# A long convolution and Haar mixing kernel: a place within the tick for each engine's part of a stage, and 14 instead of 12 products on ScalarE in the first mixing

## The chip, the cores and the metric

One core of a Trainium2 chip. The metric is the device time of the one launch in microseconds (us), the median of several runs. One execution is also recorded by the hardware profiler; all views below come from that execution.

## The reference, cut to what matters

The input is `x[4, 64, 256, 256]` in f32: 4 batches, 64 channels, images of 256 x 256. Four layers follow each other.

```
for layer in (0, 1):                       # a long convolution, each channel by itself
    k = outer(hx, hy)                      # 256 x 256 filter, from two small sine networks
    x = causal_conv2d(x, k) + x * bias     # (done by FFT in the reference)

f1  = haar2d(x)                            # layer 2: Haar transform of rows and columns
for i in (0, 1):                           # soft threshold of mixed coefficients
    f4  = conv_w[i] @ (f1 * v[i])          # mixes the 64 channels, at every position
    acc += sign(f4) * relu(abs(f4) - tau[i])
x   = haar2d_inverse(acc) + x

k   = outer(hx3, hy3)                      # layer 3: a long convolution again
out = causal_conv2d(x, k) + x * bias
```

The filter is an outer product, so a 2-D convolution is one product with a triangular Toeplitz matrix along each axis.

## The kernel before, in words

All work is cut into small stages. One **unit** of a convolution is one channel of one batch, a tile of 128 partitions x 2 x 256. Its stages are:

- `load`: the image and the first Toeplitz tile are fetched (issued on the queue of SyncE, SP).
- `a0`: `contract` multiplies with the Toeplitz matrix along one axis on TensorE into an accumulator `pa` (lines L190 and L191), and ScalarE copies the accumulator to `a` (L199).
- `y0`: the same along the other axis into `py`, and VectorE adds the input times the bias, the **residual sum** (L212).
- `a1`, `y1`: layer 1 in the same way. `a1` reads what the sum of `y0` wrote.
- `pairs`: the first Haar step on VectorE (L257, L258), into one of eight slots of `sd`; `store` sends that slot to DRAM (`keep`).
- `levels`: three events for every four channels, the remaining Haar levels along the row, in place in `sd` (VectorE, L269 and L270). The first of them overwrites what `store` reads.
- `split` and `down`: ScalarE and VectorE split the slot into two reduced-precision parts (L280, L281), TensorE applies the column transform (`pz`, L288), ScalarE copies the result (L296), and a DMA writes it to `coef`.

**Mixing** goes over 64 **groups** of 4 rows of coefficients for each batch. `mix` multiplies a group with the channel weights on TensorE (`px`, L340) into one of two accumulators and scales it by `v`. A group has 16 lines of 64 values; VectorE does the first `16 - n_act` of them in one instruction (L357), ScalarE the other `n_act`, one instruction each (L359). Then come `shrink` (ScalarE: Abs L365, Sign L366; VectorE: the subtraction of tau, L367), `signed` (VectorE: maximum with 0, times the sign, L372) and `add` (VectorE: the two products are added into `z`, L376). L367 and L372 are the **threshold steps**. `n_act` is 12 in the first three batches and 6 in the last.

**Inverse** goes over 64 channels: `fetch` (ScalarE gathers a channel of `z`, L396), `rows` (`pw` on TensorE, L403 and L404; ScalarE and VectorE split it, L406 and L407), `cols` (`pu`, L416; VectorE joins it with the kept image to `t` and `u`, L420 to L424), then layer 3 as `a3`, `y3` and the output DMA. A third of the channels of the first three batches is put off: `u` goes to DRAM (`late`), and its layer 3 is done during the last mixing (`convolution`).

The forward stages of the next batch are spread over the mixing of the present one, so a mixing stage holds both kinds of work. TensorE's work in such a tick is the product `px` and up to four contractions and one `pz`.

The order is set by a list of events: every stage of every unit has a tick, and within the tick a place.

```
    def at(tick, place, run, unit):
        events.append((tick, place, len(events), run, unit))
...
            for s, (place, stage) in enumerate([(-2.5, mix), (-3.5, shrink), (-4.1, signed), (-4.2, add)]):
                at(start + g + s, place, stage, g)
...
    for _, _, _, stage, unit in sorted(events, key=lambda e: e[:3]):
        stage(unit)
```

The sorted list is the order in which the instructions are handed to the framework. The framework keeps that as a priority; its planner may let an instruction that it takes to be ready go ahead of one that it takes to be waiting. The order on each engine is thus settled in the built program, and the engine then runs it strictly in that order, waiting where an operand is not there. Buffers are few: two accumulators for `px`, four for everything else on TensorE, two tiles each for the products `f4` and for `mag`, one for the split parts.

Of the kernel before, what the change touches and what calls it, by code (L numbers as in the profile page):

```python
# [9 lines left out]
F32 = mybir.dt.float32  # L10
# [7 lines left out]
P = 128  # L18
ROW = S + P

GT = 4
BUFS = {"res": 1, "y": 3, "co": 2}

INV_2PI = float(np.float32(1.0 / (2.0 * math.pi)))
MAGIC = float(1.5 * 2.0**23)
# [12 lines left out]
def conv_seq_kernel(ctx, tc, x, fz, fw, bias, decay, haar, haar_row, factors, vt, taut, wmix, out):  # L38
# [152 lines left out]
            nc.tensor.matmul(ps[:, m, P:], src[:, 1, m * P : (m + 1) * P], t[:, : P - 1 : -1], start=False, stop=True)  # L191

    def first(b, st, key, layer, new):
        def run(c):
            s = st[c]
            ps = bank(f"p{new}_{b}_{c}")
            contract(ps, s[key], s[layer][:, 0, :])
            a = io.tile([P, 2, S], F32, name=f"{new}_{b}_{c}", tag="mid")
            nc.scalar.copy(a, ps)  # L199
            s[new] = a  # L200

        return run

    def second(b, st, key, layer, res, new, tag, ahead=None):
        def run(c):
            s = st[c]
            if ahead is not None:
                s[ahead] = toeplitz(ahead, c, f"t{ahead}_{b}_{c}")
            ps = bank(f"p{new}_{b}_{c}")
            contract(ps, s[key], s[layer][:, 1, :])  # L210
            y = io.tile([P, 2, S], F32, name=f"{new}_{b}_{c}", tag=tag, bufs=BUFS[tag])
            nc.vector.scalar_tensor_tensor(y, s[res], bsb[:, layer, c : c + 1], ps, ALU.mult, ALU.add)  # L212
            s[new] = y

        return run

    def butterfly(b):

# [4 lines left out]

    events = []

    def at(tick, place, run, unit):
        events.append((tick, place, len(events), run, unit))

    def stream(stages, ticks):

        for unit, tick in enumerate(ticks):
            for s, stage in enumerate(stages):
                if stage is not None:
                    at(tick + s, -s, stage, unit)

    def convolutions(b, ticks, in_parts=(), border=None):

# [8 lines left out]
            nc.sync.dma_start(xt, x[b, c].rearrange("(k p) w -> p k w", p=P))  # L248
            st[c] = {"x": xt, 0: toeplitz(0, c, f"t0_{b}_{c}")}

        last_second = second(b, st, "a1", 1, "y0", "y1", "res")

        def pairs(c):
            last_second(c)
            v = st.pop(c)["y1"].rearrange("p k (w e) -> p k w e", e=2)
            t = sd[:, c % 8]
            nc.vector.tensor_add(t[:, :, 0, :], v[:, :, :, 0], v[:, :, :, 1])  # L257
            nc.vector.tensor_sub(t[:, :, 1, :], v[:, :, :, 0], v[:, :, :, 1])  # L258
# [17 lines left out]
        def split(c):  # L276

            w = parts[c] = mx.tile([P, 2, 2, S], F32R, name=f"sp_{b}_{c}", tag="sp", bufs=1)
            t = sd[:, c % 8].rearrange("p k e w -> p k (e w)")
            nc.scalar.copy(w[:, 0], t)  # L280
            nc.vector.tensor_tensor(w[:, 1], t, w[:, 0].bitcast(F32), ALU.subtract)  # L281

        def down(c):
            ps = bank(f"pz_{b}_{c}")
            flat = "p k w -> p (k w)"
            if c in in_parts:
                for i in range(2):
                    nc.tensor.matmul(  # L288
                        ps.rearrange(flat), hbr, parts[c][:, i].rearrange(flat), start=(i == 0), stop=(i == 1)
                    )  # L290
            else:
                nc.tensor.matmul(
                    ps.rearrange(flat), hbt, sd[:, c % 8].rearrange("p k e w -> p (k e w)"), start=True, stop=True
                )
            t = io.tile([P, 2, S], F32, name=f"co_{b}_{c}", tag="co", bufs=BUFS["co"])
            nc.scalar.copy(t, ps)  # L296
            nc.sync.dma_start(coef[b][:, c].rearrange("k p w -> p k w"), t)

        stream(
            [load, first(b, st, "x", 0, "a0"), second(b, st, "a0", 0, "x", "y0", "y", ahead=1), first(b, st, "y0", 1, "a1"), pairs],  # L300
            ticks,
        )
        for c, tick in enumerate(ticks):

            at(tick + 4, 3, store, c)
        for n in range(C // 4):
            end = ticks[4 * n + 3] + 4
            for s, steps in enumerate([(1,), (2, 4), (8, 16, 32, 64)]):
                at(after(end + 1 + s, n), 1, levels(steps), n)
            for j in range(4):  # L310
                if 4 * n + j in in_parts:
                    at(after(end + 3 + j, n), 2, split, 4 * n + j)
                at(after(end + 4 + j, n), 2, down, 4 * n + j)
        return after(ticks[-1] + 11, C // 4 - 1)

    def mixing(b, start, n_act):
# [18 lines left out]
        def mix(g):  # L335
            f = st[g]["f"]
            ps = psx.tile([P, 2, 2, S], F32, name=f"px_{b}_{g}", tag="mix")
            for q in range(2):
                for h in range(2):
                    nc.tensor.matmul(  # L340
                        ps[:, h, q, :],
                        f[:, q, h * P : (h + 1) * P],
                        wb.rearrange("p r n -> p (r n)"),
                        start=True,
                        stop=True,
                    )
            if g == 0:

                one, two = ps[:, :, 0, :P], ps[:, :, 0, P:]
                d = mx.tile([P, 2, P], F32, name=f"d_{b}", tag="mag")  # L350
                nc.vector.tensor_copy(d, two)
                nc.vector.tensor_sub(two, one, d)
                nc.vector.tensor_add(one, one, d)
            f4 = mx.tile([P, 16, C], F32, name=f"f4_{b}_{g}", tag="f4")
            px = ps.rearrange("p h q (r i o) -> p (h q r i) o", r=2, i=2)
            n = 16 - n_act
            nc.vector.tensor_tensor(f4[:, :n], px[:, :n], over(g, 0, n), ALU.mult)  # L357
            for j in range(n, 16):
                nc.scalar.mul(f4[:, j], px[:, j], scale(g, 0)[:, j : j + 1])  # L359
            st[g]["f4"] = f4  # L360

        def shrink(g):
            f4 = st[g]["f4"]
            mag = mx.tile([P, 16, C], F32, name=f"mag_{b}_{g}", tag="mag")
            nc.scalar.activation(mag, f4, AF.Abs)  # L365
            nc.scalar.activation(f4, f4, AF.Sign)  # L366
            nc.vector.tensor_sub(mag, mag, over(g, 1, 16))  # L367
            st[g]["mag"] = mag

        def signed(g):  # L370
            mag = st[g]["mag"]
# [4 lines left out]
            nc.vector.tensor_add(z[:, :, 4 * g : 4 * g + 4, :], parts[:, :, :, 0, :], parts[:, :, :, 1, :])  # L376

        for g in range(S // 4):
            at(start + g - 2, 0, load, g)

            for s, (place, stage) in enumerate([(-2.5, mix), (-3.5, shrink), (-4.1, signed), (-4.2, add)]):
                at(start + g + s, place, stage, g)

    def inverse(b, start, put_off):

# [11 lines left out]
        def rows(c):  # L399
            a = st[c]["z"]  # L400
            ps = psm.tile([P, 2, 2, P], F32, name=f"pw_{b}_{c}", tag="mm")
            for m in range(2):
                nc.tensor.matmul(ps[:, m, 0, :], a[:, 0, m, :], hsinv, start=True, stop=True)  # L403
                nc.tensor.transpose(ps[:, m, 1, :], a[:, 1, m, :], ident)  # L404
            w = mx.tile([P, 2, 2, 2, P], F32R, name=f"w_{b}_{c}", tag="f4")
            nc.scalar.copy(w[:, 0], ps)  # L406
            nc.vector.tensor_tensor(w[:, 1], ps, w[:, 0].bitcast(F32), ALU.subtract)  # L407
            st[c]["w"] = w
            if c not in put_off:
                st[c][2] = toeplitz(2, c, f"t2_{b}_{c}")  # L410

        def cols(c):
            ps = psm.tile([P, 2, 2, P], F32, name=f"pu_{b}_{c}", tag="mm")
            flat = "p m e w -> p (m e w)"
            for i in range(2):
                nc.tensor.matmul(  # L416
                    ps.rearrange(flat), hb, st[c]["w"][:, i].rearrange(flat), start=(i == 0), stop=(i == 1)
                )
            t = io.tile([P, 2, 2, P], F32, name=f"t_{b}_{c}", tag="res", bufs=BUFS["res"])
            nc.vector.scalar_tensor_tensor(t, st[c]["r"], 0.5, ps, ALU.mult, ALU.add)  # L420
            u = io.tile([P, 2, S], F32, name=f"u_{b}_{c}", tag="y", bufs=BUFS["y"])
# [2 lines left out]
            nc.vector.tensor_sub(v[:, :, :, 1], t[:, :, 0, :], t[:, :, 1, :])  # L424
            st[c]["u"] = u

        ends = last(b, st)
        for c in range(C):

            at(start + c, -1, fetch, c)  # L430
            at(start + c + 1, -9, rows, c)
            at(start + c + 2, -8, cols, c)
            if c in put_off:
                at(start + c + 3, -5, lambda c: nc.scalar.dma_start(late[b, c], st.pop(c)["u"]), c)
            else:
                for s, stage in enumerate(ends):
                    at(start + c + 3 + s, s - 7, stage, c)

    def last(b, st):
        return [  # L440
            first(b, st, "u", 2, "a3"),
            second(b, st, "a3", 2, "u", "y3", "co"),
            lambda c: nc.scalar.dma_start(out[b, c].rearrange("(k p) w -> p k w", p=P), st.pop(c)["y3"]),
        ]

    def convolution(which, ticks):

        for (b, c), tick in zip(which, ticks):
# [4 lines left out]
                nc.sync.dma_start(u, late[b, c])  # L453
                st[c] = {"u": u, 2: toeplitz(2, c, f"t2_{b}_{c}")}

            for s, stage in enumerate([load, *last(b, st)]):
                at(tick + s, -s, stage, c)


    def spread(begin, end, n=C):  # L460
# [17 lines left out]
    two[8](9)  # L478
    for tick, do in enumerate([constants, None, None, *three[:-1], *tables()], 4):
        if do is not None:  # L480
            at(tick, 3, lambda unit, do=do: do(), 0)

    groups = S // 4
    ready = convolutions(0, range(C), in_parts=range(C))
    ahead = C
    start = ready + 3
    for b in range(B):
        mixing(b, start, 12 if b + 1 < B else 6)
        end = start + groups + 3
        if b + 1 < B:  # L490
            ready = convolutions(b + 1, spread(ahead, end + 2), in_parts=range(C), border=end)
# [5 lines left out]

        start = max(end + C, ready + 3)
        ahead = start - 3
    for _, _, _, stage, unit in sorted(events, key=lambda e: e[:3]):  # L500
        stage(unit)


# [107 lines left out]
```

## Time and profile before

| | us |
|---|---|
| median of 3 runs | 2977.2 (2973.15 to 2978.07) |
| the profiled execution | 2975.2 |
| its span | 2973.4 |
| px of the first mixing begins | 453.5 |
| px of the last mixing ends | about 2708 |
| 453 to 883, first mixing and its border: PE, DVE, ACT busy | 418.93, 405.97, 390.40 of 430 |
| 1092 to 1558, second mixing | 460.27, 430.00, 404.26 of 466 |
| 1558 to 1766, second inverse | 207.03, 176.16, 137.86 of 208 |
| 2436 to 2725, last mixing | 280.28, 279.36, 245.02 of 289 |

PE is TensorE's matmuls, PEld its weight loads, DVE VectorE, ACT ScalarE, SP the queue of SyncE. "Busy" is the time in which at least one instruction of the engine runs; instructions that follow at once overlap at their ends, so a mean duration is longer than the step from one to the next. The granted TensorE clock is 1.00 throughout. In the waits, `A <- B: t, n, m` says that A's engine was idle for t us in n stretches, the longest m, until B released it.

### The profile page before, as it was taken

The page shows a single profiled execution, that of the slowest core. Times are in us where ns is not written, and L with a number is a line of the kernel's source. Part 1 is how long each engine was busy: PE and PEld are TensorE (multiplying, and loading weights), DVE is VectorE, ACT ScalarE, POOL GpSimd, SP SyncE. Part 2 cuts the span into 40 slices and gives each one's busy share as a digit, 9 for nine tenths or more (in the row PEclk, how much of TensorE's full clock was granted, in tenths as well). Part 3 has the DMA queues.
Part 4 walks back from the last instruction along what each step waited for, and adds up shares of the span by engine and source line. Part 5 has one row for each costly group of instructions (what it writes and reads, how often), then busy time and mean ns, then how long its engine had stood idle before and what let it go on. Part 6 is the DMA issues. An engine that isn't in the chain of part 4 may idle for free. (4 is left out here: it accounts for less than half of the span.)

```text
span 2973.4 us, 52066 instructions
## 1 busy us (share of the span) xinstructions
PE 2913.8 (98%) x16950; PEld 2615.1 (88%) x16950; DVE 2545.5 (86%) x4571; ACT 2156.9 (73%) x5014; POOL 0.2 (0%) x4
## 2 busy tenths in 40 slices
PE   8999999999999999999999999999999999999999
PEld 6898988888888898888888988888888988888998
DVE  5766768999998879999989879999998889998776
ACT  2333338999986758889986668989986768887554
POOL 0000000000000000000000000000000000000000
PEclk9999999999999999999999999999999999999999
DMA  5877777666667876776777876777777878777676
GB/s 159 247 237 226 229 228 212 203 202 207 207 196 244 250 217 200 208 216 204 208 219 244 250 225 197 209 210 211 207 216 237 256 236 235 233 230 217 212 212 186
DMA packets 562497, 649.73 MB, mean 219 GB/s; under 512 B 44369, under 2 KB 447412, under 8 KB 562100
## 3 DMA queue, kind: packets, MB, share of 16 engines
q1 hardware_dynamic: 482996, 562.07, 64.8%
q10 hardware_dynamic: 79232, 84.34, 8.0%
q8 instruction: 137, 2.24, 0.3%
q14 instruction: 132, 1.08, 0.1%
HBM read 426.77 MB, written 219.48 MB: 217 GB/s over the span
## 5 line engine op out<-in xcount | busy, mean ns | idle before, releaser
L190 PE MATMUL py<-t,a 128*128 128x256 f32 x3072 | 919.0, 381 | 8.9 <-ACT a L199 5.5
L199 ACT COPY a<-pa 128x512 f32<-128x512 f32 x768 | 477.2, 621 | 387.9 <-PE pa L191 357.2
L359 ACT ACTIVATE f<-px,vt 128x64 f32<-128x64 f32 x2688 | 582.3, 358 | 143.5 <-DVE f L357 143.4
L191 PEld LDWEIGHTS py<-t,a 128*128 128x128 f32 x3072 | 583.4, 190 | 79.3
L191 PE MATMUL py<-t,a 128*128 128x128 f32 x3072 | 590.0, 274 | 0.0
L190 PEld LDWEIGHTS py<-t,a 128*128 128x128 f32 x3072 | 500.4, 191 | 50.9 <-ACT a L199 12.4
L340 PE MATMUL px<-wb,f 128*128 128x256 f32 x2048 | 488.2, 380 | 4.9 <-ACT f L359 4.9
L340 PEld LDWEIGHTS px<-wb,f 128*128 128x128 f32 x2048 | 369.5, 190 | 47.0 <-ACT f L359 6.7
L367 DVE TENSOR_TENSOR mag<-mag,vt 128x1024 f32<-128x1024 f32 x256 | 312.4, 1220 | 28.3 <-ACT mag L365 26.9
L190 PE MATMUL pa<-t,y 128*128 128x256 f32 x1024 | 311.6, 386 | 22.4 <-DVE y L212 20.3
L406 ACT CAST w<-pw 128x512 fp32r<-128x512 f32 x256 | 150.2, 587 | 227.0 <-PE pw L404 218.9
L372 DVE SCALAR_TENSOR_TENSOR mag<-mag,f 128x1024 f32<-128x1024 f32 x256 | 311.7, 1218 | 1.9
L190 PE MATMUL pa<-t,x 128*128 128x256 f32 x1024 | 305.9, 380 | 0.4 <-issue 0.4
L365 ACT ACTIVATE mag<-f 128x1024 f32<-128x1024 f32 x256 | 293.7, 1147 | 11.0 <-DVE z L376 8.8
L366 ACT ACTIVATE f<-f 128x1024 f32<-128x1024 f32 x256 | 285.2, 1114 | 3.0
L396 ACT COPY zc<-z 128x512 f32<-128x512 f32 x256 | 282.0, 1103 | 0.7 <-ACT w L406 0.4
L281 DVE TENSOR_TENSOR sp<-sd,sp 128x512 fp32r<-128x512 f32 x256 | 176.1, 688 | 91.4 <-ACT sp L280 90.2
L190 PE MATMUL pa<-t,u 128*128 128x256 f32 x772 | 232.8, 383 | 2.9 <-PE pu L416 1.6
L420 DVE SCALAR_TENSOR_TENSOR t<-r,pu 128x512 f32<-128x512 f32 x256 | 174.9, 683 | 60.4 <-PE pu L416 57.0
L212 DVE SCALAR_TENSOR_TENSOR y<-x,bsb,py 128x512 f32<-128x512 f32 x256 | 190.1, 742 | 37.9 <-PE py L191 36.1
L212 DVE SCALAR_TENSOR_TENSOR y<-y,bsb,py 128x512 f32<-128x512 f32 x256 | 190.0, 742 | 34.2 <-PE py L191 33.1
L191 PEld LDWEIGHTS pa<-t,x 128*128 128x128 f32 x1024 | 194.6, 190 | 26.3
(67 smaller groups left out, 4458.9 us busy)
## 6 DMA issues: line engine op xcount, KB each, us to landing
t<-pad SPq DMA_DIRECT2D x768, 256.0 KB, 3.9
x<-in_x SPq DMA_DIRECT2D x256, 256.0 KB, 3.6
keep<-sd SPq DMA_DIRECT2D x256, 256.0 KB, 2.9
coef<-co SPq DMA_DIRECT2D x256, 256.0 KB, 3.3
f<-coef SPq DMA_DIRECT2D x256, 256.0 KB, 3.2
r<-keep SPq DMA_DIRECT2D x256, 256.0 KB, 3.3
out_y<-y ACTq DMA_DIRECT2D x256, 256.0 KB, 3.6
late<-u ACTq DMA_DIRECT2D x63, 256.0 KB, 2.9
```

The lines of the kernel that those rows point to most:

```text
L190: nc.tensor.matmul(ps[:, m, :], src[:, 0, m * P : (m + 1) * P], t[:, ::-1], start=True, stop=False)
L191: nc.tensor.matmul(ps[:, m, P:], src[:, 1, m * P : (m + 1) * P], t[:, : P - 1 : -1], start=False, stop=True)
L199: nc.scalar.copy(a, ps)
L212: nc.vector.scalar_tensor_tensor(y, s[res], bsb[:, layer, c : c + 1], ps, ALU.mult, ALU.add)
L281: nc.vector.tensor_tensor(w[:, 1], t, w[:, 0].bitcast(F32), ALU.subtract)
L340: nc.tensor.matmul(ps[:, h, q, :], f[:, q, h * P : (h + 1) * P], wb.rearrange("p r n -> p (r n)"), start=True, stop=True,)
L359: nc.scalar.mul(f4[:, j], px[:, j], scale(g, 0)[:, j : j + 1])
L365: nc.scalar.activation(mag, f4, AF.Abs)
L366: nc.scalar.activation(f4, f4, AF.Sign)
L367: nc.vector.tensor_sub(mag, mag, over(g, 1, 16))
L372: nc.vector.scalar_tensor_tensor(mag, mag, 0.0, st[g]["f4"], ALU.max, ALU.mult)
L396: nc.scalar.copy(a, z[:, :, :, c].rearrange("p h (i k) -> p h k i", k=2))
```

## The change

Each stage is cut into the part of each engine (`first` gives a product and a copy, `second` a product and a sum, `down` a product and `away`, `rows` loses its split to `halves`, `cols` its sums to `join`, `mix` its products with `v` to `scaled` and `scaled_too`, `shrink` loses `size` and `sign`). An event no longer has a tick and a place; it has one time, the tick plus an offset from the table `PLACE`, with offsets of their own for the last batch (`l ...`). The arithmetic is the same. Within a tick the subtraction of tau (`shrink`, 0.777) and the sign step (`signed`, 0.802) now come behind the residual sums (`y1 sum` 0.429, `y0 sum` 0.571); before, they came ahead of them. ScalarE's products are handed over in two runs, `scaled too` and `scaled rest`. `n_act` becomes a table, in which the first batch has 14 instead of 12. The levels and the split move from behind the next units' loads to offsets of 0.73. The mixing's load moves from two ticks ahead to 0.977 ahead.

```
+N_ACT = (14, 12, 12, 6)
+PLACE = {
+    "load": 0.714, "a0": 1.643, "a0 copy": 1.643, "y0": 2.571, "y0 sum": 2.571,
+    "a1": 3.5, "a1 copy": 3.5, "y1": 4.429, "y1 sum": 4.429, "pairs": 4.639, "keep": 4.929,
+    "levels": 0.73, "split": 0.734, "rest": 0.734, "down": 0.734, "away": 0.734,
+    "mix load": -0.977, "mix": 0.536, "scaled": 0.583, "scaled too": 0.583, "scaled rest": 0.584,
+    "size": 1.468, "sign": 1.476, "shrink": 1.777, "signed": 2.802, "add": 3.331,
+    "fetch": 0.414, "rows": 1.071, "halves": 1.522, "cols": 2.143, "join": 2.433,
+    "aside": 3.357, "a3": 3.47, "a3 copy": 3.471, "y3": 4.542, "y3 sum": 4.542, "out": 5.537,
...
-    def at(tick, place, run, unit):
-        events.append((tick, place, len(events), run, unit))
+    def at(time, run, unit):
+        events.append((time, len(events), run, unit))
...
+        def scaled(g):
+            px, n = st[g]["px"], 16 - n_act
+            nc.vector.tensor_tensor(st[g]["f4"][:, :n], px[:, :n], over(g, 0, n), ALU.mult)
+
+        def scaled_too(g, half):
+            px, f4 = st[g]["px"], st[g]["f4"]
+            for j in range(16 - n_act + half * (n_act // 2), 16 - (1 - half) * (n_act - n_act // 2)):
+                nc.scalar.mul(f4[:, j], px[:, j], scale(g, 0)[:, j : j + 1])
...
-        mixing(b, start, 12 if b + 1 < B else 6)
+        mixing(b, start, N_ACT[b])
```

## The prediction

> **What bounds the kernel now.** I read the page's busy times first, then busy times by stage, then the waits of the first mixing, then one stretch of the timeline.
>
> The page, part 1:
>
> ```profile
> PE 2913.8 (98%) x16950; PEld 2615.1 (88%) x16950; DVE 2545.5 (86%) x4571; ACT 2156.9 (73%) x5014; POOL 0.2 (0%) x4
> ```
>
> TensorE is the engine to beat, and the change touches none of its work. The idle 59.6 us understate what could be won, because the modelled ends of matmuls overlap. When I add up, over all matmuls, how much later one starts after the one before than the same pair usually does (the f32 128x256 passes follow at 0.216 us), I get 94 us of hold-ups: 18 in the first 100 us, 7 in the rest of the first forward stage, 20 in the first mixing and its border (453 to 883 us), 10 each in mixing two and three, 14 in the last, 15 in the four inverses. About 75 us is the most that any order could give.
>
> Busy time by stage (stretch, its length, then PE, PEld, DVE, ACT): inside the first, second and fourth mixing.
>
> ```profile
> 465.00:860.00 395.00, 385.94 (x2118) 341.78 (x2119) 379.06 (x653) 368.55 (x1059) 0.00 (x0) 1.00 0.68 203
> 1150.00:1500.00 350.00, 346.10 (x1932) 310.23 (x1931) 330.23 (x582) 317.53 (x890) 0.00 (x0) 1.00 0.71 208
> 2500.00:2700.00 200.00, 196.92 (x1062) 175.65 (x1061) 198.75 (x232) 176.73 (x420) 0.00 (x0) 1.00 0.79 234
> ```
>
> In the first mixing three engines are nearly full: PE 98%, DVE 96%, ACT 93%. In the last, DVE is full (99%), so order can do nothing there.
>
> The longest waits of the first mixing and its border (engine, line, releaser: us, times, longest):
>
> ```profile
> ACT f L359 <- DVE f L357: 30.5, 40, 3.6
> PEld pa L190 <- DVE y L212: 15.7, 21, 1.9
> ACT a L199 <- PE pa L191: 8.7, 5, 3.0
> PE pa L190 <- DVE y L212: 8.5, 15, 1.5
> ```
>
> ScalarE waits for one thing: VectorE's few products with v (L357), since its own products (L359) read the same accumulators and come behind. TensorE waits for one thing: the residual sum y0 (L212), which the contraction a1 needs. One place where both happen:
>
> ```profile
> 560.83 1.22 DVE L367 TENSOR_TENSOR mag<-mag,vt 128x1024 f32<-128x1024 f32 x1
> ...
> 561.96 0.41 DVE L357 TENSOR_TENSOR f<-px,vt 128x256 f32<-128x256 f32 x1
> ...
> 562.30 0.73 DVE L212 SCALAR_TENSOR_TENSOR y<-x,bsb,py 128x512 f32<-128x512 f32 x1
> 562.41 2.56 ACT L359 ACTIVATE f<-px,vt 128x64 f32<-128x64 f32 x12 [2.35 <-DVE f L357]
> ...
> 563.09 0.70 PE L190 MATMUL pa<-t,y 128*128 128x256 f32 x2 [1.53 <-DVE y L212]
> ```
>
> The threshold subtraction (L367) stands ahead of the products and of y0; ScalarE loses 2.35 us and TensorE 1.53.
>
> **The change part by part.** I laid the two built programs' orders side by side, engine by engine, and priced each instruction that changes places by the usual spacing to its successor in the trace.
>
> *What hardly moves.* TensorE's order is the same but for neighbours changing places near the borders and single px matmuls. Of 2194 issues on SP, 1967 keep their place and none moves over 3; the mixing's loads, nominally a tick later, are issued 6 us or more ahead of use even in the tightest case of before. So DMA: 0. Start-up, first forward stage and last inverse have the same orders on VectorE and ScalarE: 0, bounds -1 and +1 us.
>
> *First mixing, more products on ScalarE.* 64 groups x 2 products. A run of 12 takes 2.56 us, one alone about 0.36, so each further one adds 2.2/11 = 0.200; the group's busy time gives 582.3/2688 = 0.217. That is 25.6 to 27.8 us more for ScalarE. VectorE's share falls from 128x256 to 128x128; its rows are
>
> ```profile
> L357 DVE TENSOR_TENSOR f<-px,vt 128x256 f32<-128x256 f32 x192 | 80.4, 419 | 0.5 <-PE px L340 0.5
> ...
> L357 DVE TENSOR_TENSOR f<-px,vt 128x640 f32<-128x640 f32 x64 | 52.3, 817 | 1.5
> ```
>
> a slope of (817-419)/6 = 66 ns a row of 64, so 0.133 a group and 8.5 us in all. ScalarE pays three times what VectorE saves. [...]
>
> *First mixing, the order on VectorE.* y0 moves ahead by 0.54 us in the median, the products with v by 0.60; the threshold subtraction comes 0.34 later and the sign step 0.48. Stall by stall, the smaller of TensorE's hold-up for y0 and of the move ahead sums to 9.3 us. For ScalarE's waits for L357 the same sum is 16.4, and the shorter L357 adds 40 x 0.133 = 5.3: 21.7 of 30.5. What is added: y0 is now asked for sooner, and where py is not done VectorE waits with the subtraction, the levels and the next L357 behind it; y0 started 1.18 us after py in the median (0.41 in the tightest twentieth), so this is some tenths, and only for the few that move over 1.1. Four of the stage's first Haar levels (L269) come 1.13 us sooner, towards the store of `keep` they wait for (they started 3.2 to 4.1 us after its issue, and it lands after 2.9): 1.8 us of VectorE in all, out of the 8.5 saved.
>
> *What the stage gains.* TensorE's side allows 9.3 us. ScalarE's side allows less: it works or waits for L357 without a gap (368.55 + 26.5 = 395.0 of 395), so its account is +25.6 minus the waits that go: between 21.7 (+3.9 us) and all 30.5 (-4.9). Waits under 0.15 us are not listed, so a little more than -4.9 is possible. I take **-5**, near the end where the waits go: in the new order L357 stands ahead of the preceding group's subtraction in most groups, and that was what held it. Ends: -9.3 and +3.9.
>
> *Borders.* Where the first forward stage meets the mixing, three y0 or parts sums move 0.36 to 0.66 ahead of hold-ups of 0.17, 0.30 and 1.33: -0.8. At 868 to 878 us a ScalarE copy of a1 moves 0.96 ahead (hold-up 0.88) and two more move: -1.7. Together **-2.5**, ends -2.5 and 0.
>
> *Second and third mixing.* Here the built order does not do what the title says: y0 stands 0.20 us *later* in the mean, behind one more small level step. Per 62 us there are two hold-ups: one of 0.4 to 0.9 us for y0 (0.10 worse), and one of 0.29 that goes, since L357 of the group before stands ahead of its sign step and ScalarE's Abs comes sooner. A copy of a0 moves 2.35 us back behind the products, with 2.19 us to spare and the products starting earlier: 0 to +0.16. Over 12 periods 12 x (0.10 + 0.05 - 0.29) = -1.7, taken as **-2**; ends -4 and, if the copy of a0 is late in every period and passes it on, +4.
>
> *Inverses.* In the first ten channels of each, the left-over levels come sooner and u and w later (u of channel 3 by 1.9 us with 0.6 to spare, of 4 by 0.6 with none, w of 7 by 1.7 with 0.7). The same work is then missing further on, where it held TensorE up by 0.7. Net 0 to +2 in each of three: **+2** in all, ends 0 and +6.
>
> *Last mixing.* VectorE is full and its work the same: **0**, ends -2 and +2.
>
> Sum: -5 - 2.5 - 2 + 2 = -7.5 us. The profiled execution took 2975.2 us (span 2973.4, 1.8 around it), which gives 2967.7; the median of the runs, 2977.2, lies 2.0 above the profiled one, so **2970 us**, 0.24% down. All low ends together make -19, all high ends +17.
>
> **The rivals.** Differences within 0.2% (6 us) I count as no change; that is about what a measurement of this kernel can tell.
>
> *No change.* ScalarE's new products eat exactly the waits that go (25.6 of 30.5 us), so the first mixing stays, and borders, middle mixings and inverses make -2.5: 2975. For it: the orders differ little outside the first mixing, and the account of ScalarE lies on both sides of nothing. Against it: TensorE's hold-ups for y0 are real and y0 does move.
>
> *Slower: ScalarE becomes the bound of the first mixing.* It would have 368.55 + 62 x 0.400 = 393.4 us of work in a stretch that lasts 395. VectorE, the fullest of the two there, reaches 96% with its waits; at 96% ScalarE needs 409.8, 14.8 more. With the borders' -2.5 that is 2989. It decides as soon as fewer than 25.6 us of ScalarE's waits disappear. Against it: in the last mixing VectorE does reach 99%, so a full engine need not lose 4%. [...]
>
> **Chances.** Forecast (gain by over 0.2%) 0.40; no change 0.32; slower by over 0.2% 0.28, nearly all of it ScalarE's rival, a little the high ends of the inverses. The range goes from all low ends together (2977.2 - 18.8 = 2958, rounded outwards to 2957) up to the slower rival, 2990.
>
> **What would show it.** Right: in the first mixing ScalarE's waits for L357 fall from 30.5 to under 8, ScalarE is busy over 97%, TensorE's waits for y0 fall from 8.5 to under 3, and the last px of that stage comes some 5 us sooner; middle mixings within 2 us each; inverses 0 to 1 us longer each. Wrong: L357 waits above 10 us, or new waits of py for the copies of a0 (L199) in the first mixing, which would mean that ScalarE passes its load on to TensorE; middle mixings that change by over 4 us would mean that small moves cascade, which my move-against-slack sums leave out.

## The result, and the profile after

The changed kernel takes 2973.15 us (median of 12 runs, 2970.57 to 2979.72), the kernel before 2976.16 us beside it (12 runs, 2971.97 to 2978.81). The ratio is 0.9995, interval 0.9987 to 1.0003: no difference that this measurement can tell, a gain of 3.0 us in the medians where 7.2 was forecast, and the first rival's case. The profiled execution took 2972.79 us with a span of 2971.0, against 2975.2 and 2973.4.

The page of the changed kernel, part 1:

```profile
PE 2905.9 (98%) x16950; PEld 2615.2 (88%) x16950; DVE 2529.6 (85%) x4571; ACT 2183.4 (73%) x5142; POOL 0.2 (0%) x4
```

ScalarE has the 128 new instructions (64 groups x 2) and 26.5 us more busy time; VectorE has 15.9 us less.

Busy time by stage, changed kernel (stretch, length, then PE, PEld, DVE, ACT):

```profile
465.00:860.00 395.00, 388.53 (x2126) 341.68 (x2125) 373.84 (x654) 390.75 (x1182) 0.00 (x0) 1.00 0.68 203
1150.00:1500.00 350.00, 345.95 (x1939) 311.55 (x1940) 331.45 (x582) 318.38 (x892) 0.00 (x0) 1.00 0.71 210
2500.00:2700.00 200.00, 195.08 (x1058) 175.08 (x1058) 199.19 (x233) 178.62 (x426) 0.00 (x0) 1.00 0.80 233
```

In the first mixing ScalarE goes from 368.55 to 390.75 of 395 us (98.9%), VectorE from 379.06 to 373.84. The other two rows are as before within 2 us.

Waits of the first mixing and its border, changed kernel (engine, line, releaser: us, times, longest). L434 is the old L357, L439 the old L359, L279 the residual sum (L212), L262 the copy of an accumulator (L199), L248 and L249 the contraction (L190, L191), L415 `px` (L340):

```profile
...
PEld py L248 <- ACT a L262: 8.2, 20, 0.9
ACT a L262 <- PE pa L249: 8.0, 5, 2.8
PEld pa L248 <- DVE y L279: 7.3, 17, 2.0
ACT f L439 <- DVE f L434: 7.2, 5, 3.4
...
PE pa L248 <- DVE y L279: 2.8, 5, 1.6
PEld px L415 <- ACT f L439: 2.6, 3, 1.1
...
PE py L248 <- ACT a L262: 2.1, 5, 0.5
```

ScalarE's wait for VectorE's product has gone from 30.5 to 7.2 us, TensorE's for y0 from 8.5 to 2.8. What has grown is TensorE waiting for ScalarE: for the copies of a0 (8.2 on the weight load and 2.1 on the matmul, against the two rows below), and for the products (2.6, not in the list before). The kernel before:

```profile
PEld py L190 <- ACT a L199: 3.0, 7, 0.9
...
PE py L190 <- ACT a L199: 1.1, 2, 0.7
```

One such place, from the changed kernel's timeline:

```profile
610.15 2.95 ACT L439 ACTIVATE f<-px,vt 128x64 f32<-128x64 f32 x14
...
611.29 1.89 PE L415 MATMUL px<-wb,f 128*128 128x256 f32 x8
...
612.90 0.68 ACT L262 COPY a<-pa 128x512 f32<-128x512 f32 x1
...
613.63 0.70 PE L248 MATMUL py<-t,a 128*128 128x256 f32 x2 [0.45 <-ACT a L262]
```

The copy of a0 stands behind a run of 14 products, and the matmuls of py wait 0.45 us for it. The run is in one piece: the two halves of ScalarE's part lie next to each other in the built order.

Stage lengths read from the trace (from the first `px` of a batch to its first `pw`, and so on), with the hold-ups of TensorE in each as the prediction counts them:

| stage | before, us (hold-ups) | after, us (hold-ups) |
|---|---|---|
| start, 100 us | 100.0 (18.4) | 100.0 (18.7) |
| first forward stage | 353.5 (7.3) | 353.3 (6.7) |
| first mixing | 429.4 (19.5) | 427.4 (17.1) |
| first inverse | 209.2 (6.3) | 207.9 (6.3) |
| second mixing | 466.7 (9.8) | 466.7 (8.5) |
| second inverse | 207.2 (3.8) | 208.1 (6.0) |
| third mixing | 466.4 (9.5) | 466.4 (8.1) |
| third inverse | 203.9 (4.4) | 203.6 (6.7) |
| last mixing | 289.2 (14.5) | 289.6 (12.3) |
| last inverse | 244.0 (0.3) | 244.0 (0.3) |

The sum of the differences is -2.5 us, the spans differ by 2.4. The same stage with the same built order scatters by some 2 us between executions: in five programs that share the changed kernel's order of the second mixing (the changed kernel, n12, n16, cheap and levA1 below, run on at least three chips) it took 466.7, 466.2, 466.5, 467.8 and 468.8 us. So only stage differences above that are read below.

### The profile page after: what moved, and what is told of

It reads as the page before. It is cut to its first block, busy times and chain, and to the rows that moved or that the text cites. A ratio compares the mean times of both kernels' runs of the same rounds, so it can differ in the third digit from the quotient of the medians.

```text
span 2971.0 us, 52173 instructions
## 1 busy us (share of the span) xinstructions
PE 2905.9 (98%) x16950; PEld 2615.2 (88%) x16950; DVE 2529.6 (85%) x4571; ACT 2183.4 (73%) x5142; POOL 0.2 (0%) x4
## 5 line engine op out<-in xcount | busy, mean ns | idle before, releaser
L248 PE MATMUL py<-t,a 128*128 128x256 f32 x3072 | 920.4, 381 | 11.7 <-ACT a L262 6.3
L262 ACT COPY a<-pa 128x512 f32<-128x512 f32 x768 | 485.8, 633 | 374.7 <-PE pa L249 338.9
L439 ACT ACTIVATE f<-px,vt 128x64 f32<-128x64 f32 x2816 | 619.9, 391 | 113.8 <-DVE f L434 113.2
L249 PEld LDWEIGHTS py<-t,a 128*128 128x128 f32 x3072 | 583.4, 190 | 79.4
L249 PE MATMUL py<-t,a 128*128 128x128 f32 x3072 | 590.0, 274 | 0.0
L248 PEld LDWEIGHTS py<-t,a 128*128 128x128 f32 x3072 | 498.4, 191 | 57.4 <-ACT a L262 18.1
L415 PE MATMUL px<-wb,f 128*128 128x256 f32 x2048 | 486.6, 380 | 6.4 <-ACT f L439 6.4
L415 PEld LDWEIGHTS px<-wb,f 128*128 128x128 f32 x2048 | 369.2, 190 | 48.3 <-ACT f L439 8.5
L248 PE MATMUL pa<-t,y 128*128 128x256 f32 x1024 | 310.0, 385 | 16.7 <-DVE y L279 15.4
L443 ACT ACTIVATE mag<-f 128x1024 f32<-128x1024 f32 x256 | 299.8, 1171 | 20.4 <-DVE z L458 19.6
L248 PE MATMUL pa<-t,x 128*128 128x256 f32 x1024 | 305.8, 380 | 1.1 <-issue 1.1
L248 PE MATMUL pa<-t,u 128*128 128x256 f32 x772 | 231.0, 381 | 10.2 <-issue 9.5
L279 DVE SCALAR_TENSOR_TENSOR y<-x,bsb,py 128x512 f32<-128x512 f32 x256 | 190.8, 745 | 39.3 <-PE py L249 39.2
L279 DVE SCALAR_TENSOR_TENSOR y<-y,bsb,py 128x512 f32<-128x512 f32 x256 | 190.3, 744 | 38.0 <-PE py L249 37.8
L249 PEld LDWEIGHTS pa<-t,y 128*128 128x128 f32 x1024 | 194.5, 190 | 26.4
```

Of the source, the lines that this page charges most:

```text
L248: nc.tensor.matmul(ps[:, m, :], src[:, 0, m * P : (m + 1) * P], t[:, ::-1], start=True, stop=False)
L262: nc.scalar.copy(a, s["p" + new])
L415: nc.tensor.matmul(ps[:, h, q, :], f[:, q, h * P : (h + 1) * P], wb.rearrange("p r n -> p (r n)"), start=True, stop=True,)
L443: nc.scalar.activation(mag, st[g]["f4"], AF.Abs)
```

## The experiments

Theory: the changed places put L434 and y0 ahead, and ScalarE's two further products take back most of what that gives. Rivals: the products alone make the difference, and the places do something else; or the Haar levels, which the places move forward, cost what the rest gains. A ratio is always against the kernel before, run beside it; stage lengths are from one profiled execution each.

**Products and places apart.** The changed kernel with 12 products, and the kernel before with 14.

```
n12:  N_ACT = (12, 12, 12, 6)                         # changed kernel, was (14, 12, 12, 6)
b14:  mixing(b, start, (14, 12, 12, 6)[b])            # kernel before, was 12 in batch 0
```

> The changed kernel with 12 products a group on ScalarE in the first mixing, as before, and everything else kept; the planner then puts y0 0.5 us and the products with v 0.6 us later again in that mixing. Theory A (the two further products eat what the waits gave back): ScalarE drops from 99% to about 93% busy there, TensorE's holds for the copies of a0 go back from 8.2 to about 3 us, its holds for y0 return to 12 to 16 us, and the stage, 429.4 us before and 427.4 now, comes out at 428 to 430: 0 to 2 us above the changed kernel. Rival B (ScalarE's load is the cost, and the order by itself is the gain): the stage falls to 422 to 425 us and the kernel gains 3 to 5 us on the changed one.

> The kernel before with 14 products a group on ScalarE in the first mixing, its own stage order kept. Theory A (order and products belong together: without the earlier L357 the waits for it, 30.5 us, do not go): ScalarE needs 368.55 + 25 + some 20 us of waits in 395, so the stage is 8 to 20 us longer and the kernel 0.3 to 0.7% slower. Rival B (the smaller product on VectorE frees it whatever the order): within 2 us of the kernel before.

Measured: n12 1.0000 (0.9991 to 1.0009), 2975.63 us; b14 0.9984 (0.9975 to 0.9993), 2969.37 us, the two on one chip. Waits of the first mixing, b14, which still has the old line numbers:

```profile
...
PEld py L190 <- ACT a L199: 8.1, 21, 0.8
...
PEld pa L190 <- DVE y L212: 6.6, 19, 0.8
ACT f L359 <- DVE f L357: 5.6, 4, 3.4
```

and n12:

```profile
ACT f L439 <- DVE f L434: 26.3, 36, 3.6
PEld pa L248 <- DVE y L279: 16.2, 23, 1.9
PE pa L248 <- DVE y L279: 8.7, 19, 1.5
```

The waits follow the number of products and hardly the places. With the new places and 12 products ScalarE waits 26.3 us for L434 and TensorE 8.7 for y0, much as before the change (30.5 and 8.5). With the old places and 14 products the first wait is 5.6. The order of b14's instructions tells why: though no place was changed, the planner puts y0 0.56 us ahead in the median and L357 0.60, and the threshold subtraction 0.33 back, which is the whole shift (0.54, 0.60 and 0.34) that I had put down to the places. Sorting TensorE's hold-ups in the first mixing by what is held up shows the exchange:

| kernel | stage, us | for y0 | for py | for px |
|---|---|---|---|---|
| before (12, old places) | 429.4 | 15.0 | 2.9 | 0.1 |
| n12 (12, new places) | 427.2 | 15.2 | 0.9 | 0.1 |
| b14 (14, old places) | 424.6 | 6.2 | 5.7 | 1.6 |
| after (14, new places) | 427.4 | 7.5 | 6.6 | 2.2 |

With the old places two products more take 8.8 us off the holds for y0 and add 4.3 for py and px, and the stage is 4.8 us shorter. With the new places they take off 7.7 and add 7.8, and the stage stays. That is where the gain of the earlier y0 went. The stage of b14 with the same built order took 426.4 us in a second program (b14all below) and 425.0 in a third (thr, but for six places on VectorE), the changed kernel's order 427.5 in a14all: so with 14 products the new places cost some 1 to 3 us here, of the size of the scatter. For n12, Theory A had the waits right and the stage 0.8 us too long at its low end; Rival B fell. For b14 both theories fell: it gains, by 0.16%.

**ScalarE with all 16 products.**

```
n16:  N_ACT = (16, 12, 12, 6)                         # changed kernel; L434 is left out where no line is left for it
```

> The changed kernel with all 16 products of a group on ScalarE in the first mixing, VectorE's product left out there. ScalarE then has 390.75 + 62 x 0.4 = 415.5 us of work in a stretch that now lasts 395. Theory A (ScalarE is the bound of that mixing now): the stage grows by at least 20 us and the kernel by 20 to 30 us (+0.7 to +1.0%). Rival B (ScalarE has slack that busy time hides, for the waits for L434, 7.2 us, are gone altogether): under +12 us.

Measured: 1.0065 (1.0052 to 1.0078), 2993.76 us; the first mixing takes 446.4 us, 19.0 more than with 14. Its busy time from 465 to 860 us, and its waits over the whole stage (L440 there is the changed kernel's L439):

```profile
465.00:860.00 395.00, 376.23 (x2037) 324.98 (x2037) 347.38 (x568) 393.40 (x1243) 0.00 (x0) 1.00 0.65 196
```

```profile
PEld px L415 <- ACT f L440: 27.9, 25, 1.8
...
PE px L415 <- ACT f L440: 18.1, 24, 1.4
```

Now ScalarE is the bound: `px` waits for its products, 18.1 us on the matmuls. An estimate from the spacing of its instructions (0.196 us from a product to what follows, 0.465 from a copy of an accumulator, 0.52 from a split, 0.96 from Abs and from Sign, each times its count) puts its work in this stage at some 377, 402 and 427 us with 12, 14 and 16 products, and at the new places the stage takes 427.2, 427.4 and 446.4. The first 25 us cost nothing on balance (the built order changed with them), of the next 25 the stage pays 19. So 98.9% busy was still no bound; b14, whose stage is shorter, is fuller still:

```profile
465.00:860.00 395.00, 390.38 (x2143) 344.14 (x2142) 377.33 (x660) 392.72 (x1194) 0.00 (x0) 1.00 0.68 205
```

Theory A was right in kind; the stage grew by 1 us less than its low end.

**The same split with less work on ScalarE.**

```
cheap:  if j < 13: nc.scalar.mul(f4[:, j], px[:, j], scale[j])          # as in the changed kernel
        elif j == 13: nc.scalar.mul(f4[:, 13:], px[:, 13:], scale[13])  # one instruction for lines 13 to 15
```

> The changed kernel with lines 13 to 15 of a group in the first mixing done by one ScalarE instruction with the factor of line 13 (the factors of lines 14 and 15 are left out), so that VectorE's product has two lines as in the changed kernel, and ScalarE 12 instructions as before: about 0.1 us a group more than the kernel before, and 0.3 less than the changed one. The planner then puts y0 0.67 us and L434 0.69 us later again. Theory A (the order is the gain, and the planner makes it from ScalarE's load): holds for y0 come back to 7 us or more, waits for L434 to over 20, and the stage is 425 to 429 us although ScalarE has 20 us less to do. Rival B (ScalarE's load is what eats the gain): waits for a0 vanish and the stage falls to 418 to 423 us.

Measured: 0.9998 (0.9989 to 1.0007), stage 425.7 us. ScalarE is busy 376.62 of 395 us, 14 less than in the changed kernel. Its waits for L434 are back at 21.4, and the holds for y0 at 9.3 by the count of the table. Theory A: the planner's order, which comes from the work it sees on ScalarE, decides the waits, since VectorE's product is as short here as in the changed kernel and they came back all the same. The load taken away did not shorten the stage beyond the scatter, and py still waits for the copies of a0 (7.0 us on the weight load), so Rival B fell. How much of b14's gain is the order and how much VectorE's shorter product was not tried at the old places.

**14 products in the second and third mixing too.**

```
b14all:  mixing(b, start, 14 if b + 1 < B else 6)     # kernel before
a14all:  N_ACT = (14, 14, 14, 6)                      # changed kernel
```

> The kernel before with 14 products a group on ScalarE in the first three mixings, its stage order kept. In the first mixing 14 products alone took 4.8 us off the stage (429.4 to 424.6) and put y0 0.57 us ahead. Theory A (the products do it, through the planner, which puts L357 and y0 ahead when ScalarE has more to do): in mixings two and three ScalarE has 386 + 26 = 412 us of work in 466, so it is no bound; the holds for y0, most of 9.8 us each, fall by 3 to 6, and the kernel gains 6 to 12 us more: 2957 to 2964. Rival B (the first mixing is a case of its own, because only there ScalarE and VectorE are both full): the two mixings stay within 1.5 us, 2968 to 2971.

> The changed kernel with 14 products a group on ScalarE in the first three mixings. In the built order y0 then comes 0.11 us sooner in mixings two and three and L434 0.15, against 0.57 and 0.61 in the first mixing of the kernel before. Theory A (what counts is how far y0 moves): 1 to 4 us gain in the two together, 2969 to 2972. Rival B (the shorter product on VectorE is worth something by itself, 64 x 0.133 = 8.5 us of VectorE a mixing): 3 us or more in each, 2964 to 2968.

Measured: 1.0021 (1.0011 to 1.0030) and 1.0036 (1.0022 to 1.0049). All theories fell: the two mixings grow, to 473.7 and 472.4 us, and 473.5 and 475.8. Waits from 1150 to 1500 us, kernel before:

```profile
ACT f L359 <- DVE f L357: 29.2, 34, 2.2
...
DVE mag L367 <- ACT mag L365: 4.0, 6, 0.7
PE pa L190 <- DVE y L212: 3.2, 5, 1.7
```

b14all:

```profile
ACT f L359 <- DVE f L357: 17.3, 20, 2.4
...
DVE mag L367 <- ACT mag L365: 8.6, 12, 1.3
PE pa L190 <- DVE y L212: 8.5, 12, 1.2
```

and a14all, against 1.6 and 4.0 for the same two rows in the changed kernel:

```profile
DVE mag L450 <- ACT mag L443: 9.5, 12, 1.3
...
PE pa L248 <- DVE y L279: 7.7, 12, 1.1
```

In b14all ScalarE loses 12 us of waits for L357, as hoped, and is busy 330.57 of 350, no bound. But its longer run of products delays Abs (L365); VectorE now waits 8.6 us for it in front of the threshold subtraction, with y0 queued behind, and TensorE's waits for y0 rise from 3.2 to 8.5. The same edit that gains in the first mixing loses 6 to 9 us in each of the others. That the waits for Abs cause the later y0, and not the planner's other moves beside them, is read from the rows and was not tried by itself. For it speaks a14all: its order has y0 0.1 us sooner than the changed kernel's, where b14all's has it 0.1 us later than the kernel before, and both pay the same waits.

**The threshold steps back at their old places.** The subtraction at 1.5 stands behind the sum of y1 (0.429 in the tick) and ahead of that of y0 (0.571), the sign step at 2.42 ahead of both. That is the order of the kernel before: there the sign step came ahead of both sums, but the subtraction ahead of y0's alone, not of y1's.

```
thr:  "shrink": 1.5, "signed": 2.42                   # changed kernel, was 1.777 and 2.802
```

> The changed kernel with the threshold steps of VectorE back in front of the residual sums (subtraction from place 1.777 to 1.5, the second step from 2.802 to 2.42). The built order of the first mixing then hardly differs (y0 0.01 us, the subtraction 0.08), but in mixings two and three y0 comes 0.33 us sooner, L434 0.41 and the subtraction 0.5, and the Haar levels 2.9 later. Theory A (the levels ahead of y0 make the holds of the middle mixings, and the place of the threshold steps only matters through them): the first mixing stays within 1.5 us, mixings two and three gain 2 to 5 us each, 2963 to 2969. Rival B (threshold steps behind the sums help TensorE, as the change has it): mixings two and three lose 1 to 4 us each, 2975 to 2981.

Measured: 1.0018 (1.0009 to 1.0026), 2982.82 us. The first mixing takes 425.0 us (2.4 less than the changed kernel, about the scatter), the second 471.2 and the third 471.7 (4.5 and 5.3 more). The second mixing, 1150 to 1500 us, thr:

```profile
ACT f L439 <- DVE f L434: 36.1, 38, 1.9
...
PEld py L248 <- ACT a L262: 4.9, 5, 1.0
```

In the changed kernel these two rows have 30.5 and 1.3 us. ScalarE stands longer in front of its products, with copies of a0 behind it, and py waits. Rival B, slightly larger than it said: in the changed kernel the new threshold places are worth some 5 us in each of these mixings, where the change as a whole moved nothing. If the parts add up, something else in it costs as much there. But the edit also let the planner set the Haar levels 2.9 us later, so the 5 us are not those of the threshold steps alone.

**The levels.** The suspect was the place of the Haar levels, 0.73, which sets them in front of the threshold steps of their tick. Three ways to put them back:

```
lev1:   "levels": 1.0                                           # was 0.73
levA:   "levels": 1.0, "split", "rest", "down", "away": 1.004   # was 0.73 and 0.734
levC:   levels at 1.0, split, rest, down and away at 1.734, in all but the last two groups of a batch
```

> The changed kernel with the Haar levels put back from place 0.73 to 1.0 of their tick (all stages); VectorE then has levels about 5 us later, y0 about 0.3 us earlier in the mixings, and w, t and u 0.2 us earlier in the inverses. Theory A (the earlier levels are what makes TensorE wait in the inverses): the holds of the three inner inverses, 6.3, 6.0 and 6.7 us, fall to about 4 each, and the kernel gains 3 to 6 us. Rival B (the holds there come from the copies of w on ScalarE and not from levels): the inverses stay within 1 us, and the kernel within 2 us of the changed one.

> The changed kernel with the Haar levels and the splits, column transforms and copies behind them from places 0.73 and 0.734 to 1.0 and 1.004, so that levels come behind the threshold steps of their tick again, each split still behind its levels. In the built order y0 then comes 0.18 us sooner in mixings two and three, 0.09 in the first, and the levels 1.2 and 0.5 later. Theory A (the levels ahead of y0 and of L434 cost what the threshold steps gave): mixings two and three, 466.7 and 466.4 us, lose 1.5 to 4 us each, holds for y0 fall from 7 to about 4, and the kernel gains 3 to 8 us on the changed one. Rival B (the levels gained in the run with place 1.0 only because the last chain of levels no longer stood ahead of the first split of its group): the mixings stay within 1 us.

> The changed kernel with the levels at place 1.0 and the splits, column transforms and copies of every channel but the last eight of a batch one whole tick later (1.734). Every split stays behind its levels, and levels get a tick more before the first split needs them. Built order: y0 0.43 us sooner in the first mixing and 0.71 in mixings two and three, splits 5.4 later. Theory A (a level step's due time is what pushes it in front of y0): conv0 and the three mixings lose 2 to 5 us each, the kernel comes to 2955 to 2964. Rival B (the levels were not the cause, the missing dependence was): within 3 us of the changed kernel; or the splits, later now, hold up the column transforms and the stages grow.

lev1 leaves out part of the computation, which its expectation does not say: with 1.0 against 0.734 the split of every fourth channel stands ahead of the last chain of levels of its group (steps 8 to 64), and its column transform takes sums without that chain. All instructions are still there. Measured: lev1 0.9941 (0.9928 to 0.9955), levA 0.9989 (0.9980 to 0.9998), levC 0.9989 (0.9980 to 0.9997). lev1's second and third mixing take 462.4 and 461.8 us, and the first forward stage 351.0; the second mixing, 1150 to 1500 us, lev1:

```profile
...
PEld pa L248 <- DVE y L279: 1.9, 6, 0.5
...
PE pa L248 <- DVE y L279: 0.3, 1, 0.3
```

TensorE's wait for y0 is nearly gone (4.0 in the changed kernel). But with the dependence kept, levA has 468.6 and 468.9 us there, levC 468.1 and 467.8, with TensorE's wait for y0 at 4.2 and 4.1. So Theory A of both fell, and Rival B holds in kind (levA's two mixings are 1.9 and 2.5 us longer, where it allowed 1): the later place alone does not pay there, and what sets lev1 apart is the missing dependence. The likely reason, not tried by itself: in lev1 the eight small steps may not start until that split has read its slot, so the planner cannot draw them forward in front of y0. lev1's gain of some 16 us on the changed kernel is not to be had by this edit. What levA and levC gain, they gain in the first mixing: 424.1 and 423.4 us against 427.4, though levA's order took 425.6 in a second program.

My expectation for lev1, the inverses, was wrong on both sides: the holds of the second and third stay (6.3 and 6.7 us), while the kernel gains. That does not clear the levels, for the edit left one of them where it does harm. The second inverse of the changed kernel:

```profile
1586.98 0.69 DVE L327 TENSOR_TENSOR sd<-sd 128x512 f32<-128x512 f32 x1 [1.89 <-DMA keep<-sd]
...
1588.44 0.67 PE L248 MATMUL pa<-t,u 128*128 128x256 f32 x2 [1.36 <-issue]
```

The level waits 1.89 us for its store, u is queued behind it and done at 1588.34, and a3, which reads u, starts 0.10 us later. In lev1 the same level still stands in front of that u and waits 2.28 us.

**Mixed places by stage.**

```
levC0:  levC, and in the first mixing "shrink": 1.5, "signed": 2.42
levA1:  late = 0.27 if b < 2 else 0.0                 # levA's places for the first two batches alone
```

> As the run before, and in the first mixing alone the threshold steps at their old places, in front of the residual sums (1.5 and 2.42). Undone everywhere, the threshold places took 2.4 us off the first mixing and added 4.5 and 5.3 in mixings two and three. Theory A (in the first mixing ScalarE is full, so the subtraction that frees its next product should go first): 1 to 3 us less than the run before. Rival B (the 2.4 us was scatter between executions of equal stages): within 1 us.

> The changed kernel with levels, splits, column transforms and copies at places 1.0 and 1.004 for the first two batches alone, whose forward stages run in conv0 and in the first mixing; from the third batch on 0.73 and 0.734 as in the changed kernel. The built order of the first mixing is then that of the run with these places everywhere, the order of mixings two and three that of the changed kernel. Theory A (each order has its own price in each mixing, and the prices add up by stage): the first mixing comes to 424.1 us (427.4 in the changed kernel), mixings two and three stay at 466.5, and the kernel is 3 us faster than the changed one: ratio to the kernel before 0.9980 to 0.9990. Rival B (the 3 us of the first mixing is scatter between executions): the first mixing lies at 426 to 428 and the ratio at 0.9992 to 1.0002.

Measured: levC0 0.9993 (0.9984 to 1.0001), first mixing 424.7 us against levC's 423.4; levA1 0.9989 (0.9980 to 0.9998), first mixing 425.6, second 468.8. levC0's Theory A fell: the first mixing did not get shorter. Otherwise both are undecided: the pieces are of the size of the scatter, and levA1's second mixing, whose order is the changed kernel's, is the slowest of the five named above.

The fastest kernel that computes everything is b14, the old places with 14 products in the first mixing: 0.16% (0.07 to 0.25) below the kernel before. Its interval overlaps with those of levA, levA1, levC and levC0, and by a little with the changed kernel's.

## Why the prediction was right or wrong

The time lies in the range given, but that range was 33 us wide. The gain of over 0.2%, to which I gave the largest chance (0.40), did not come; no change (0.32) did.

- **ScalarE's waits for L357, and its load.** Said: under 8 us and over 97% busy. Measured: 7.2 and 98.9%. In a run the products start 0.196 us apart in both kernels, so two more cost 0.39 us.
- **TensorE's waits for y0.** Said: under 3 us. Measured: 2.8.
- **First mixing, the term that failed.** Said: -5 us. Measured: -2.0, which is about the scatter. Two things were wrong in it. I took the value "near the end where the waits go"; 23.3 of the 30.5 us went, near the other end (21.7). And I had written that new waits of py for the copies of a0 would mean that ScalarE passes its load on to TensorE: they came, so y0's relief of 7.5 us was met by 3.7 more for py and 2.1 for px.
- **Its cause.** I put the earlier L357 and y0 down to the changed places. b14 and n12 show that the number of products moves them, through the planner; the places by themselves (n12) took 4.2 us off the first wait and nothing off the second.
- **ScalarE's account as a bound.** The prediction took it that ScalarE "works or waits for L357 without a gap", so that fewer than 25.6 us of vanished waits would lengthen the stage. Only 23.3 vanished, and it did not grow: by the spacing of its instructions ScalarE had an estimated 377 us of work in 429.4. The recorded busy time hid that slack: the records of one product last far longer than the 0.196 us between two starts, and longer in the changed kernel (mean 381 ns before, 506 after), so a late start of the next instruction need not show as idle time (rows in the last section). In the changed kernel the product at 500.79 us is recorded for 0.78 us, the next instruction starts 0.60 us after it, and no idle time is listed between the two. The slower rival had its point of decision too early: it lies between 14 and 16 products.
- **Borders.** Said: -2.5. Measured: -0.2 in the first forward stage and -1.3 in the first inverse, both within the scatter.
- **Second and third mixing.** Said: -2, within 2 each. Measured: 0.0 and 0.0, but not because little happened: thr shows that without the new threshold places each would be about 5 longer. What takes that back is not settled; the place of the levels alone does not do it, since levA's and levC's mixings (467.8 to 468.9) were not shorter.
- **Inverses.** Said: +2 in all, from left-over levels. The holds rose by 2.2 and 2.3 us in the second and third; the lengths changed by +0.9 and -0.3. The holds fit in size, and so does the cause in part: the changed kernel's second inverse has two holds of over 1.5 us which the kernel before has not, and one of them lies behind a level that waits for its store.
- **Last mixing.** Said: 0. Measured: +0.4.
- **A full engine relieved.** In the second mixing of the kernel before VectorE is busy 330.23 of 350 us (ScalarE 317.53, the weight loads 310.23). b14all relieves it to 322.19 by shorter products, and the stage grows by 7.0 us: what counted there, as far as the rows tell, was the wait for Abs in front of y0.

## What to carry to other kernels

Before crediting a gain to a hand-set place, build the program with each part of the edit alone and compare the orders: where a planner settles them, a changed instruction count can move more than the places do. Here ScalarE at 98.9% (first mixing, changed kernel) was not the bound, and at 94% (second mixing, b14all, 330.57 of 350 us) its Abs held VectorE up for 8.6 us, with y0 queued behind; so try both one step up and one stage along before spreading an edit. When a variant is much faster than its neighbours, look for a dependence that it lost.

## What the runs showed of the hardware

A high recorded busy share of ScalarE did not say that it set the time. At 93% (n12) and 98.9% (the changed kernel) the first mixing took 427.2 and 427.4 us, at 99.4% (b14) 424.6, and only at 99.6% (n16), with some 25 us of further work, 446.4. The recorded busy time overstates the work: products that start 0.196 us apart are recorded at 381 ns each in the kernel before and 506 in the changed one, and the spacing of all its instructions gives an estimated 402 us of work in a stage of 427.4 us (94%) where the records say 98.9%. ScalarE's products from 465 to 860 us, the kernel before and the changed one (busy us, mean ns of one):

```profile
L359 ACT ACTIVATE f<-px,vt 128x64 f32<-128x64 f32 x744 | 161.4, 381 | 26.5 <-DVE f L357 26.5
```

```profile
L439 ACT ACTIVATE f<-px,vt 128x64 f32<-128x64 f32 x866 | 197.5, 506 | 4.2 <-DVE f L434 3.6
```

Equal instruction orders in a stage took between 466.2 and 468.8 us in different executions, so a single profile tells nothing here below about 2.5 us in 467.

VectorE and ScalarE ran in the built order: in the kernel before all 4571 and 5013 instructions of the two (the load of ScalarE's table aside) start in the trace in the order of the built program, line by line, and their waits lie between them: 30.5 us of ScalarE for L357 in the first mixing alone.
